# A graph network of four layers: two stages change the order of their work

## The chip, the cores and the metric

The kernel runs on one core of a Trainium2 chip. The core has five engines with a queue of instructions each: TensorE (PE; the loading of its weights is listed apart as PEld), VectorE (DVE), ScalarE (ACT), GpSimd (POOL) and SyncE (SP), which here only issues transfers. The engines work side by side and wait for one another by semaphores. The metric is the device time of one execution in microseconds (us); lower is better.

## The reference

There are 16 graphs of 1024 nodes with 256 features each, and a dense matrix `adj` of 1024 x 1024 weights per graph. Each of the four layers normalizes the features of a node (mean 0, variance 1), cuts them off below 0, computes something from the result `h` and `adj`, and adds that to `x`:

```python
# layer 0: attention whose weights are adj * exp(e_i + f_j + a_b), divided by their row sums
x = x + (u / u.sum(-1)) @ (h @ W_w.T + W_b)          # u = adj * exp(...)
# layer 1: graph convolution
d = (adj.sum(-1) + 1e-5) ** -0.5
x = x + (d[:, :, None] * adj * d[:, None, :]) @ (h @ weight) + bias
# layer 2: a gated recurrence over the 1024 nodes of a graph, one node after the other
# layer 3: neighbour sums, a wide inner layer with RMS norm and silu
agg = epsilon * h + adj @ h
t = agg @ W1 + b1                                     # inner width 1024
t = silu(t * rsqrt(mean(t * t) + 1e-6) * rms_weight)
x = x + t @ W2 + b2
```

All arithmetic is float32. A float32 product on TensorE is made of two instructions, so that counts of matmuls in the profile are twice those in the code.

## The kernel before

The program has three parts, one after the other: layers 0 and 1 together, layer 2, layer 3. Only the first and the last are changed; layer 2 takes the middle of the time and is the same in both versions. Between the parts, `x2_d`, `he_d`, `heT_d` and `hn_d` carry results through HBM. A graph is called a batch below. `NT` = 8 blocks of 128 nodes, `DC` = 2 halves of the features, `HC` = 8 blocks of the inner width.

**Layers 0 and 1.** `load` brings x (1 MB) and the transposed `adj` (`at`, 4 MB in four transfers) of a batch. `prepare` takes the statistics of x (`stats`, lines 128 to 136), forms the cut-off rows `q` (L176), the products `f` (L178), the exponentials `g` (L182) and scales q (L187). `layer_0` first multiplies `at` by g and by ones (`pd`, L196), which gives the row sums; then come the neighbour sums of q (`sums`, L152, 64 instructions with four results `pa`), the products with the weights (L214) and the addition to x (L215). `reshape` takes the statistics of the new x and forms the rows `h1` (L144). `layer_1` has the neighbour sums of h1, the products (L251), the addition (L252), the statistics of that and the rows `h2`, which leave for HBM. `turn` transposes h2 (L268). The loop interleaves these: in step i stand layer 0 of batch i, the transposes of batch i-2, and layer 1 of batch i-1, and in the pauses between the four neighbour sums of the latter the statistics of batch i (`reshape`) and the preparation of batch i+1.

**Layer 3.** For each batch: load x, hn and `at`; add epsilon to the diagonal of `at` (GpSimd, L683); x + hn (L684); normalize and cut off (L76 to L83); add b2 to x (GpSimd, L687); neighbour sums (L693), which come out with the features on partitions (`ag`). Then twice, for 512 nodes: the inner layer with the nodes on partitions (`ph`, L706), b1 added (L709), squares with their sum (L711), the root mean square (`rms`, L68), the scaling (L717), the transposes back (`pt`, L721) with silu (L722), and the products with W2 (L726) added to x (L727).

**What sets the order.** The kernel is written in a framework with a planner that orders the instructions before the program runs. By its own estimates of times it gives each engine the first instruction in program order whose inputs and buffers are there; so an instruction can overtake earlier ones of its engine that have to wait. In the chip's run that order is fixed, and each engine works through it strictly in order. Tiles are buffers with a name and a pool; a name has a fixed number (`bufs`) of them, which go round. `mv` has 2, `s6` 4 (L132), `pa` 2, `pmm` 2 in the first part.

Of the kernel before, what the change touches and what calls it, by code (L numbers as in the profile page):

```python
# [9 lines left out]
F32 = mybir.dt.float32  # L10
# [6 lines left out]
P = 128  # L17
# [21 lines left out]
def gnn_stack(ctx: ExitStack, tc: tile.TileContext, a: dict, out: bass.AP):  # L39
# [51 lines left out]


    def layers_0_1():
        with ExitStack() as st:
            wp = st.enter_context(tc.tile_pool(name="w01", bufs=1))
            big = st.enter_context(tc.tile_pool(name="big01", bufs=1))
# [41 lines left out]
            def normed(x, scale, mv, name, bufs):  # L138

                shift = small.tile([P, NT], F32, name="shift")  # L140
                nc.vector.scalar_tensor_tensor(shift, mv[:, :, 0], -1.0, scale, op0=ALU.mult, op1=ALU.mult)
                h = big.tile([P, NT, D], F32, name=name, bufs=bufs)
                for t in range(NT):
                    nc.scalar.activation(h[:, t], x[:, t], AF.Relu, bias=shift[:, t : t + 1], scale=scale[:, t : t + 1])  # L144
                return h

            def sums(at, h, ag):

                def part(n0, c):
                    pa = psum.tile([P, 512], F32, name="pa")  # L150
                    for mt in range(NT):
                        nc.tensor.matmul(pa, h[:, mt, c * P : (c + 1) * P], at[:, mt, n0 : n0 + 512],  # L152
                                         start=mt == 0, stop=mt == NT - 1)
                    if c == 0:
                        nc.scalar.copy(ag[:, c, n0 : n0 + 512], pa)
                    else:
                        nc.vector.tensor_copy(ag[:, c, n0 : n0 + 512], pa)  # L157
                return [lambda n0=n0, c=c: part(n0, c) for n0 in (0, 512) for c in range(DC)]

            at, x, q, g, h1, h2, dis = {}, {}, {}, {}, {}, {}, {}  # L160

            def load(b):
                x[b] = big.tile([P, NT, D], F32, name="x", bufs=4)
                nc.sync.dma_start(x[b], rows(a["x"][b]))
                at[b] = big.tile([P, NT, N], F32, name="at", bufs=3)
                for t in range(0, NT, 2):
                    nc.sync.dma_start(at[b][:, t : t + 2], rows(a["adjT"][b])[:, t : t + 2])

            def prepare(b):

                mv, rs = stats(x[b])
                yield
                q[b] = big.tile([P, NT, D], F32, name="q")
                f = small.tile([P, NT], F32, name="f")
                for t in range(NT):
                    nc.vector.tensor_scalar(q[b][:, t], x[b][:, t], mv[:, t, 0:1], 0.0, op0=ALU.subtract, op1=ALU.max)  # L176
                    junk = small.tile([P, D], F32, name="junk")
                    nc.vector.scalar_tensor_tensor(junk, q[b][:, t], rs[:, t : t + 1], v[:, :D],  # L178
                                                   op0=ALU.mult, op1=ALU.mult, accum_out=f[:, t : t + 1])
                    nc.gpsimd.tensor_tensor(x[b][:, t], x[b][:, t], vec["W_b"], ALU.add)  # L180
                g[b] = gs[b % 2]
                nc.scalar.activation(g[b][:, :, 0], f, AF.Exp, bias=v[:, D : D + 1])  # L182
                yield
                rg = small.tile([P, NT], F32, name="rg")
                nc.vector.tensor_mul(rg, rs, g[b][:, :, 0])
                for t in range(NT):
                    nc.scalar.activation(q[b][:, t], q[b][:, t], AF.Copy, scale=rg[:, t : t + 1])  # L187
                yield

            def layer_0(b, between):  # L190
                ds = big.tile([P, N], F32, name="ds")
                for n0 in (0, 512):
                    pd = psum.tile([P, 512], F32, name="pd")
                    for mt in range(NT):
                        k = mt % 4
                        nc.tensor.matmul(pd[32 * k : 32 * (k + 1)], g[b][:, mt], at[b][:, mt, n0 : n0 + 512],  # L196
                                         start=mt < 4, stop=mt >= 4)
                    nc.scalar.copy(ds[:, n0 : n0 + 512], pd)
                ag = big.tile([P, DC, N], F32, name="ag", bufs=2)
                for part in sums(at[b], q[b], ag):  # L200
                    part()
                    if between:
                        between.pop(0)()
# [6 lines left out]
                nc.vector.tensor_copy(deg, pn[:, :, 1])  # L210
                for nt in range(NT):
                    po = psum.tile([P, D], F32, name="pmm")
                    for c in range(DC):
                        nc.tensor.matmul(po, ag[:, c, nt * P : (nt + 1) * P], w0[:, c], start=c == 0, stop=c == DC - 1)  # L214
                    nc.vector.scalar_tensor_tensor(x[b][:, nt], po, rc[:, nt : nt + 1], x[b][:, nt],  # L215
                                                   op0=ALU.mult, op1=ALU.add)

                dis[b] = inv_sqrt(small, deg, DEG_EPS, [P, NT], "dis")
# [7 lines left out]
                return safe  # L226

            def reshape(b, safe):

# [5 lines left out]
                mv, rs = stats(x[b])  # L235
                rd = small.tile([P, NT], F32, name="rd")
                nc.vector.tensor_mul(rd, rs, dis[b])
                h1[b] = normed(x[b], rd, mv, "h1", 2)
                for t in range(NT):
                    nc.gpsimd.tensor_tensor(x[b][:, t], x[b][:, t], vec["bias"], ALU.add)  # L240

            def layer_1(b, between):
                ag = big.tile([P, DC, N], F32, name="ag", bufs=2)
                for part in sums(at[b], h1[b], ag):
                    part()
                    if between:
                        between.pop(0)()
                for nt in range(NT):
# [3 lines left out]
                    nc.vector.scalar_tensor_tensor(x[b][:, nt], po, dis[b][:, nt : nt + 1], x[b][:, nt],  # L252
                                                   op0=ALU.mult, op1=ALU.add)
                nc.gpsimd.dma_start(rows(x2_d[b]), x[b])

                mv, rs = stats(x[b])
                h2[b] = normed(x[b], rs, mv, "h2", 1)
                nc.gpsimd.dma_start(rows(he_d[b]), h2[b])

            def turn(b):  # L260

                hT = big.tile([P, DC, N], F32, name="hT")

                def part(c):
                    for t0 in range(0, NT, 4):
                        pt = psum.tile([P, 512], F32, name="pt")
                        for t in range(4):
                            nc.tensor.transpose(pt[:, t * P : (t + 1) * P], h2[b][:, t0 + t, c * P : (c + 1) * P], ident)  # L268
# [4 lines left out]
                    if c == DC - 1:  # L273
                        nc.gpsimd.dma_start(heT_d[b], hT)
                return [lambda: part(0), lambda: part(1)]

            nothing = lambda: None
            load(0)
            for _ in prepare(0):
                pass  # L280
            for i in range(B + 2):
                if i + 1 < B:
                    load(i + 1)
                turns = [nothing] + turn(i - 2) if i >= 2 else []
                if i < B:
                    safe = layer_0(i, turns)
                for part in turns:
                    part()
                between = []
                if i < B:  # L290
                    between.append(lambda: reshape(i, safe))
                if i + 1 < B:
                    rows_of = prepare(i + 1)
                    between += [lambda: next(rows_of)] * 3
                if 1 <= i <= B:
                    layer_1(i - 1, between)
                for part in between:
                    part()
# [350 lines left out]

    def layer_3():  # L650
        with ExitStack() as st:
# [8 lines left out]
            nc.sync.dma_start(w2, a["W2"].rearrange("(c p) e -> p c e", p=P))  # L660
            rw = wp.tile([P, HC], F32, name="rw")
            with nc.allow_non_contiguous_dma(reason="weights, once"):
                nc.sync.dma_start(rw, a["rms_weight"].rearrange("(c p) -> p c", p=P))
            b1 = wp.tile([P, H], F32, name="b1")
            nc.sync.dma_start(b1, bcast_row(a["b1"], H))  # L665
# [7 lines left out]
            NH = 512  # L673
            for b in range(B):
                at = big.tile([P, NT, N], F32, name="at")
                x = big.tile([P, NT, D], F32, name="x")
                hn = big.tile([P, NT, D], F32, name="hn", bufs=1)
                nc.sync.dma_start(x, rows(x2_d[b]))
                nc.sync.dma_start(hn, rows(hn_d[b]))  # L679
                for t in range(0, NT, 2):  # L680
                    nc.sync.dma_start(at[:, t : t + 2], rows(a["adjT"][b])[:, t : t + 2])  # L681
                for t in range(NT):
                    nc.gpsimd.tensor_tensor(at[:, t, t * P : (t + 1) * P], at[:, t, t * P : (t + 1) * P], eye, ALU.add)  # L683
                nc.vector.tensor_add(x, x, hn)  # L684
                h = ln_relu(small, big, x)
                for t in range(NT):
                    nc.gpsimd.tensor_tensor(x[:, t], x[:, t], b2, ALU.add)  # L687
                ag = big.tile([P, DC, N], F32, name="ag", bufs=1)
                for n0 in range(0, N, NH):
                    for c in range(DC):  # L690
                        pa = psum.tile([P, NH], F32, name="pa")
                        for mt in range(NT):
# [89 lines left out]
```

## Time and profile before

| | |
|---|---|
| median of 3 runs | 6928.25 us (6926.89 to 6928.35) |
| profiled execution, its own time | 6928.25 us |
| its span in the profile | 6926.5 us |
| TensorE busy, instructions | 6482.0 us (94%), 28325 |
| layers 0 and 1, first `pd` to last transpose | 27.57 to 1327.6 us |
| layer 3, first neighbour sum to the end | 5332.75 to 6926.5 us |
| mean granted TensorE clock | 0.968 |

The profile is that of one execution. Times in its views count from the start of the span. A group line has the line of the code and the engine, the operation, the tiles written and read, shapes and count; then busy time, the mean of one in ns, and the idle time of the engine before it with what ended it. A line in order of time begins with start and duration in us. The duration of one matmul overlaps with the next one, so the rate of a row of them is read from the starts. A line of windows gives, for each stretch, the busy time of the engines, the clock that TensorE was granted as a fraction of the full one, the busy share of the 16 DMA engines and GB/s.

### The profile page before, as it was taken

To read this page: it belongs to the slowest core of one execution; us is meant where nothing else is said; L and a number is where in the kernel's file an instruction comes from. 1 tells how busy PE (TensorE), PEld (TensorE's weight loads), DVE (VectorE), ACT (ScalarE), POOL (GpSimd) and SP (SyncE) were. 2 spreads that over 40 slices of the span, in tenths; PEclk is the share of its full clock that TensorE was granted. 3 is DMA by queue.
4 is the path that set the end of the run, shared out by engine and by line. 5 is a ranking of instruction groups with operands and counts; after the bars stand their busy time and mean duration, and the time that the engine had idled before them with its cause. 6 is when DMAs were issued, how large, how long until landed. Compare 5 with 4: busy or idle time off the path is not lost. (4 is left out here: it accounts for less than half of the span.)

```text
span 6926.5 us, 72473 instructions
## 1 busy us (share of the span) xinstructions
PE 6482.0 (94%) x28325; PEld 4703.9 (68%) x28325; DVE 2475.9 (36%) x5926; ACT 1447.6 (21%) x3211; POOL 894.6 (13%) x1299
## 2 busy tenths in 40 slices
PE   7999999679999999999999999999998999999998
PEld 3455545378878878788788788788785555555555
DVE  4444444213333333333333333333333233323332
ACT  1211222102212212112112122122122222222222
POOL 2222322110000000100100100000001111111110
PEclk9999999899999999999999999999999999999999
DMA  3322222371131132221221222211003122212210
GB/s 120 121 105 99 98 97 98 95 210 56 62 87 49 60 88 63 65 72 52 63 74 61 73 65 62 82 49 49 22 6 109 65 79 85 69 66 78 85 55 13
DMA packets 477363, 520.77 MB, mean 75 GB/s; under 512 B 30208, under 2 KB 428800, under 8 KB 474752
## 3 DMA queue, kind: packets, MB, share of 16 engines
q1 hardware_dynamic: 461056, 447.93, 20.2%
q0 software_dynamic: 15872, 67.18, 2.6%
q8 instruction: 256, 4.19, 0.3%
q14 instruction: 179, 1.47, 0.1%
HBM read 431.10 MB, written 83.95 MB: 74 GB/s over the span
## 5 line engine op out<-in xcount | busy, mean ns | idle before, releaser
L401 PEld LDWEIGHTS pb<-ab,hb 128*128 128x128 f32 x3648 | 522.8, 195 | 89.1 <-issue 34.3
L401 PE MATMUL pb<-ab,hb 128*128 128x128 f32 x3648 | 533.8, 280 | 50.2 <-DMA hb<-he_d 30.5
L551 PE MATMUL pa<-wh,r 128*128 128x256 f32 x2080 | 494.2, 380 | 0.0
L152 PE MATMUL pa<-at,h 128*128 128x512 f32 x1024 | 459.1, 603 | 34.9 <-DVE ag L157 34.9
L693 PE MATMUL pa<-at,h 128*128 128x512 f32 x1024 | 444.3, 595 | 31.5 <-ACT h L83 31.5
L726 PE MATMUL pa<-w,hT 128*128 128x256 f32 x2048 | 468.1, 384 | 0.0
L539 ACT ACTIVATE r<-pr 128x256 f32<-128x256 f32 x520 | 199.2, 383 | 1230.1 <-PE pr L536 1217.5
L706 PE MATMUL ph<-w,ag 128*128 128x512 f32 x1024 | 452.7, 593 | 0.0
L152 PE MATMUL pa<-at,q 128*128 128x512 f32 x1024 | 448.4, 594 | 0.0
L551 PEld LDWEIGHTS pa<-wh,r 128*128 128x128 f32 x2080 | 387.2, 191 | 74.7 <-issue 22.9
L726 PEld LDWEIGHTS pa<-w,hT 128*128 128x128 f32 x2048 | 385.3, 193 | 46.5
L152 PEld LDWEIGHTS pa<-at,h 128*128 128x128 f32 x1024 | 195.2, 193 | 272.0 <-issue 223.9
L693 PEld LDWEIGHTS pa<-at,h 128*128 128x128 f32 x1024 | 195.6, 191 | 270.9 <-issue 267.4
L536 PE MATMUL pr<-x,wh 128*128 128x256 f32 x1568 | 372.7, 380 | 0.0
L543 PE MATMUL pz<-wh,x 128*128 128x256 f32 x1568 | 370.5, 379 | 0.0
L562 DVE TENSOR_TENSOR w<-w,hc 128x256 f32<-128x256 f32 x520 | 236.2, 454 | 370.8 <-ACT hc L561 370.8
L540 DVE TENSOR_TENSOR r<-r,x 128x256 f32<-128x256 f32 x392 | 167.0, 426 | 542.8 <-ACT r L539 541.7
L152 PEld LDWEIGHTS pa<-at,q 128*128 128x128 f32 x1024 | 191.5, 190 | 236.9 <-issue 236.9
L706 PEld LDWEIGHTS ph<-w,ag 128*128 128x128 f32 x1024 | 191.2, 190 | 214.8 <-issue 214.0
L543 PEld LDWEIGHTS pz<-wh,x 128*128 128x128 f32 x1568 | 298.4, 190 | 40.0
L536 PEld LDWEIGHTS pr<-x,wh 128*128 128x128 f32 x1568 | 292.3, 191 | 43.5 <-issue 3.3
L561 ACT ACTIVATE hc<-pa 128x256 f32<-128x256 f32 x520 | 196.2, 383 | 538.4 <-PE pa L551 538.3
(154 smaller groups left out, 9573.8 us busy)
## 6 DMA issues: line engine op xcount, KB each, us to landing
at<-in_adjT SPq DMA_DIRECT2D x128, 1024.0 KB
ab<-in_adj SPq DMA_DIRECT2D x128, 512.0 KB
x<-in_x SPq DMA_DIRECT2D x16, 1024.0 KB
x_d<-x POOLq DMA_DIRECT2D x16, 1024.0 KB, 7.7
he_d<-h POOLq DMA_DIRECT2D x16, 1024.0 KB, 8.6
heT_d<-hT POOLq DMA_DIRECT2D x16, 1024.0 KB, 4.2
he<-heT_d SPq DMA_DIRECT2D x16, 1024.0 KB
hb<-he_d SPq DMA_DIRECT2D x16, 1024.0 KB
```

The lines of the kernel that those rows point to most:

```text
L152: nc.tensor.matmul(pa, h[:, mt, c * P : (c + 1) * P], at[:, mt, n0 : n0 + 512], start=mt == 0, stop=mt == NT - 1)
L401: nc.tensor.matmul(pb[:, c], hb[:, j, c * P : (c + 1) * P], ab[:, j], start=j == jts[0], stop=j == jts[-1])
L536: nc.tensor.matmul(prs[e], wh[:, c, e * P : (e + 1) * P], x[:, c], start=False, stop=c == DC - 1)
L539: nc.scalar.activation(r[:, e], prs[e], AF.Sigmoid)
L540: nc.vector.tensor_mul(r[:, e], r[:, e], x[:, e])
L543: nc.tensor.matmul(pz[:, g], x[:, c, g * GR : (g + 1) * GR], wh[:, c, D : 2 * D], start=False, stop=g == G2 - 1 and c == DC - 1)
L551: nc.tensor.matmul(pcs[g], r[:, c, g * GR : (g + 1) * GR], wh[:, c, 2 * D :], start=False, stop=c == DC - 1)
L561: nc.scalar.activation(hc[:, g], pcs[g], AF.Tanh)
L562: nc.vector.tensor_mul(w[:, g], w[:, g], hc[:, g])
L693: nc.tensor.matmul(pa, h[:, mt, c * P : (c + 1) * P], at[:, mt, n0 : n0 + NH], start=mt == 0, stop=mt == NT - 1)
L706: nc.tensor.matmul(ph, ag[:, c, (t0 + t) * P : (t0 + t + 1) * P], w1[:, c, e * 512 : (e + 1) * 512], start=c == 0, stop=c == DC - 1)
L726: nc.tensor.matmul(po, hT[:, k, t * P : (t + 1) * P], w2[:, k], start=k == 0, stop=k == HC - 1)
```

## The change

Two parts are changed. In layers 0 and 1 the interleaving is taken out: one loop over the batches does everything for a batch in order. `x`, `at`, `q`, `ag` and the rest have two buffers each, and x1 and x2 are tiles of their own. The operations and their shapes stay the same.

In layer 3, `inner` computes the inner layer with its features on partitions, so that nothing has to be transposed; b1 and the RMS weight become a column per block. The mean over the inner width is then one over partitions and blocks: ScalarE squares each block, GpSimd adds the eight blocks up (`ss`), TensorE sums that over the partitions by a product with a column of ones (`mean`), and spreads the reciprocal root over the partitions by transposes of a broadcast column (`spread`). VectorE multiplies, ScalarE applies silu (`apply`). The neighbour sums of the next batch stand in four pieces between these, and loads and preparation run two batches ahead.

```diff
@@ layers_0_1 @@
-            big = st.enter_context(tc.tile_pool(name="big01", bufs=1))
+            big = st.enter_context(tc.tile_pool(name="big01", bufs=2))
...
+            for b in range(B):
+                at = big.tile([P, NT, N], F32, name="at")
+                x = big.tile([P, NT, D], F32, name="x")
+                nc.sync.dma_start(x, rows(a["x"][b]))
                 for t in range(0, NT, 2):
+                    nc.sync.dma_start(at[:, t : t + 2], rows(a["adjT"][b])[:, t : t + 2])
...
+                mv, rs = stats(x)
+                q = big.tile([P, NT, D], F32, name="q")
...
+                ag = summed(at, q)
...
+                x1 = big.tile([P, NT, D], F32, name="x1")
...
+                mv, rs = stats(x1)
                 rd = small.tile([P, NT], F32, name="rd")
+                nc.vector.tensor_mul(rd, rs, dis)
+                h = normed(x1, rd, mv, "h")
...
+                ag = summed(at, h)
+                x2 = big.tile([P, NT, D], F32, name="x2")
...
+                nc.gpsimd.dma_start(rows(x2_d[b]), x2)
...
+                mv, rs = stats(x2)
+                h = normed(x2, rs, mv, "h")
+                nc.gpsimd.dma_start(rows(he_d[b]), h)
                 hT = big.tile([P, DC, N], F32, name="hT")
...
-            for i in range(B + 2):
-                if i + 1 < B:
-                    load(i + 1)
-                turns = [nothing] + turn(i - 2) if i >= 2 else []
-                if i < B:
-                    safe = layer_0(i, turns)
...
-                if 1 <= i <= B:
-                    layer_1(i - 1, between)
...
@@ layer_3 @@
-            b1 = wp.tile([P, H], F32, name="b1")
-            nc.sync.dma_start(b1, bcast_row(a["b1"], H))
+            b1 = wp.tile([P, HC], F32, name="b1")
...
+            def load(b):
+                x[b] = big.tile([P, NT, D], F32, name="x", bufs=3)
+                hn[b] = big.tile([P, NT, D], F32, name="hn", bufs=1)
...
+            def prepare(b):
+                for t in range(NT):
+                    nc.gpsimd.tensor_tensor(at[b][:, t, t * P : (t + 1) * P], at[b][:, t, t * P : (t + 1) * P], eye, ALU.add)
+                nc.vector.tensor_add(x[b], x[b], hn[b])
+                h[b] = ln_relu(small, big, x[b])
+                for t in range(NT):
+                    nc.gpsimd.tensor_tensor(x[b][:, t], x[b][:, t], b2, ALU.add)
...
+            def inner(ag, n0, between):
+
+                hh = big.tile([P, HC, NH], F32, name="hh")
+                ss = small.tile([P, NH], F32, name="ss")
+                for k in range(HC):
+                    ph = psum.tile([P, NH], F32, name="ph")
+                    for c in range(DC):
+                        nc.tensor.matmul(ph, w1[:, c, k * P : (k + 1) * P], ag[:, c, n0 : n0 + NH],
+                                         start=c == 0, stop=c == DC - 1)
+                    sq = ss if k == 0 else small.tile([P, NH], F32, name="sq")
+                    nc.scalar.activation(sq, ph, AF.Square, bias=b1[:, k : k + 1])
+                    nc.vector.tensor_scalar(hh[:, k], ph, b1[:, k : k + 1], None, op0=ALU.add)
+                    if k:
+                        nc.gpsimd.tensor_tensor(ss, ss, sq, ALU.add)
+                    if k in between:
+                        between[k]()
+                return hh, ss
+
+            def norm(hh, ss):
+
+                got = {}
+
+                def mean():
+                    pq = psum.tile([P, NH // P], F32, name="pq", bufs=1)
+                    for n in range(NH // P):
+                        nc.tensor.matmul(pq[:, n : n + 1], ss[:, n * P : (n + 1) * P], ones[:, 0:1], start=True, stop=True)
+                    got["rms"] = inv_sqrt(small, pq, RMS_EPS, [P, NH // P], "rms", mul=1.0 / H)
+
+                def spread():
+                    pr = psum.tile([P, NH], F32, name="pr", bufs=1)
+                    for n in range(NH // P):
+                        nc.tensor.transpose(pr[:, n * P : (n + 1) * P], got["rms"][:, n : n + 1].to_broadcast([P, P]), ident)
+                    got["pr"] = pr
+
+                def apply(quarter):
+                    for k in (2 * quarter, 2 * quarter + 1):
+                        nc.vector.tensor_mul(hh[:, k], hh[:, k], got["pr"])
+                        nc.scalar.activation(hh[:, k], hh[:, k], AF.Silu, scale=rw[:, k : k + 1])
+                return mean, spread, apply
...
+                hh0, ss0 = inner(ag, 0, {})
+                mean0, spread0, apply0 = norm(hh0, ss0)
+                hh1, ss1 = inner(ag, NH, {1: mean0, 4: spread0})
+                mean1, spread1, apply1 = norm(hh1, ss1)
+                parts = [lambda: None] * 4
+                if b + 1 < B:
+                    ag, parts = sums(b + 1)
+                for k in range(4):
+                    apply0(k)
+                parts[0]()
+                mean1()
+                parts[1]()
+                spread1()
+                outer(b, hh0, 0, apply1)
+                parts[2]()
+                if b + 2 < B:
+                    prepare(b + 2)
+                parts[3]()
+                outer(b, hh1, NH)
+                nc.gpsimd.dma_start(rows(out[b]), x[b])
```

## The prediction

> **What bounds the kernel now.** I read the page's busy shares first, then the windows of one steady batch in layers 0/1 and one in layer 3, then the order in time on TensorE, then the groups.
>
> ```profile
> PE 6482.0 (94%) x28325; PEld 4703.9 (68%) x28325; DVE 2475.9 (36%) x5926; ACT 1447.6 (21%) x3211; POOL 894.6 (13%) x1299
> 602.41:681.35 78.94, 76.48 (x259) 40.09 (x258) 37.00 (x110) 15.95 (x33) 21.64 (x24) 1.00 0.28 107
> 5532.94:5631.92 98.98, 93.78 (x322) 56.51 (x321) 32.60 (x64) 25.74 (x58) 13.99 (x20) 0.97 0.22 75
> ```
>
> TensorE sets the time. In the windows the columns are stretch, length, busy time of PE, PEld, DVE, ACT, POOL, then clock and DMA. A batch takes 78.94 us in layers 0/1, with TensorE 97% busy at clock 1.00, and 98.98 us in layer 3 at 0.97. So layers 0/1 have almost nothing to win and much to lose; layer 3 has its transposes and gaps to win. TensorE in time order shows what an uninterleaved batch costs. The kernel's own first batch is one:
>
> ```profile
> 62.93 7.45 PE L214 MATMUL pmm<-w,ag 128*128 128x256 f32 x32
> 70.21 0.27 PE L231 MATMUL pt<-ident,safe 128*8 128x128 f32 x1
> 90.97 5.18 PE L196 MATMUL pd<-at,gs 128*32 128x512 f32 x32 [20.48 <-ACT gs L182]
> 96.08 27.73 PE L152 MATMUL pa<-at,q 128*128 128x512 f32 x64
> ...
> 641.41 7.11 PE L251 MATMUL pmm<-w,ag 128*128 128x256 f32 x32
> 648.45 3.64 PE L196 MATMUL pd<-at,gs 128*32 128x512 f32 x32
> ```
>
> After batch 0's layer 0, TensorE idles 20.48 us until batch 1's exp (gs) is done. In the steady state the same `pd` follows the last product with no gap. Why did nothing run ahead? VectorE:
>
> ```profile
> 47.69 0.69 DVE L157 COPY ag<-pa 128x512 f32<-128x512 f32 x1 [19.97 <-PE pa L152]
> 61.42 0.69 DVE L157 COPY ag<-pa 128x512 f32<-128x512 f32 x1 [13.04 <-PE pa L152]
> 72.42 0.38 DVE L133 BATCH_NORM_STATS2 s<-x 128x6 f32<-128x256 f32 x1
> ```
>
> The transfers of x[1] had ended by about 52 us (the DMA strip is at 0 from there), VectorE idled, yet batch 1's statistics start only behind batch 0's second ones at 71 us. The planner does fill gaps out of program order elsewhere, so this is a buffer: `s6` (4 buffers) and `mv` go round in program order, and later statistics queue behind earlier ones.
>
> **What the skill says.** "SBUF — State Buffer", Who interferes with whom: VectorE collides with GpSimd only with two SBUF inputs or in a 2-port mode. The trace agrees: L709 (one PSUM input) takes 689 ns under GpSimd work, 691 without; L178 (two SBUF inputs) 1237 against 474. "TensorE: Matmul & The Clock Gate", Part 1: an idle window of about 3.4 us halves the clock until about 3.4 us of work have passed. The windows agree: 0.50 from 73.6 to 91.0 us, 0.54 from 91.0 to 94.4, then 1.00; `pd` then takes 5.11 us to its successor instead of 3.57, so a long stall costs 1.5 us more. "Perfetto Trace Analysis", Optimization Strategy: consistent bubbles can mean no buffer for the next tile; that is my reading of 71 us.
>
> **Part 1, layers 0/1 go back to one batch after the other.** Statistics are now, in program order, x, x1, x2 of batch b, then x of b+1, all through the 4 buffers of `s6`. So x of b+1 can't be prepared before x2 of b has its statistics, after b's last product. Two stalls appear per batch.
>
> Stall A, layer 0 to layer 1: last L215, statistics, power on GpSimd (1.66), shift, first ACT row. Batch 0 shows it: L214 ends 70.4, the rows start at 74.73 and the first takes 0.5: 4.8 us, plus 1.5 of clock = 6.3. The first matmuls of b+1 can't fill it: they need the exp that comes later.
>
> Stall B, layer 1 to the next batch: 1.3 us until x2's statistics are done; then what the start of the kernel shows undisturbed, from first statistics (12.89) to `pd` (27.57), 14.7; added 0.6 for x2's power input and shift on VectorE, 1.3 for two 0.69 us hT copies, about 1.1 for a DMA issue on GpSimd (0.94) that holds VectorE up: 19.0. From above, the 20.48 just shown contains a heavier GpSimd load (8 bias adds). I keep 16.5 to 21.5. The 16 transposes of h lie inside B.
>
> Period: pd 5.1 + sums 27.55 + pn 1.70 + products 7.44 + A 6.3 + sums 27.47 + products 7.0 + B 19.0 = 101.6 us. The first batch starts at 27.57 as now; its last product ends 27.57 + 83.6 + 15 x 101.6 = 1635.2, against 1317.2 now: **+318 us**, 80% between 275 and 355. Loads stay hidden: `at` goes from 3 buffers to 2, but its buffer frees at the end of the sums of b-1, some 90 us before use, and 4 MB land in 11 us (the `eye` adds follow its quarters every 2.5). Layer 2's first loads wait for the last heT_d in both; what follows is unmoved, apart from the order layer 3's few weights come in (512 KB of b1 less, under 3 us).
>
> **Part 2, layer 3.** Durations on TensorE per batch now: sums 27.47, ph 2 x 13.75, products 128 x 0.2159 = 27.63; 64 transposes x 0.109 = 7.0; the rest to 98.98, 9.4, is waits and half clock. Removed: the transposes, both waits for `rms` (work of the next batch stands there), ACT's accumulator reads. Added on TensorE: 8 one-column products of 2 instructions at 0.106 (rate of L206) 1.7, and 8 transposes 0.9. Floor: 27.47 + 27.5 + 27.63 + 2.6 = 85.2.
>
> Other engines per k of `inner` (1.72 us of TensorE): ACT Square 0.6, VectorE bias 0.69, GpSimd one 128x512 add.
>
> ```profile
> L423 POOL TENSOR_TENSOR ao<-ao,dv 128x512 f32<-128x512 f32 x28 | 35.6, 1270 | 182.0 <-DMA ao<-in_adj 176.2 <-PE pb L427 5.8
> L687 POOL TENSOR_TENSOR x<-x,b 128x256 f32<-128x256 f32 x128 | 94.5, 771 | 8.5 <-DVE h L81 8.5
> L684 DVE TENSOR_TENSOR x<-x,hn 128x2048 f32<-128x2048 f32 x16 | 36.8, 2303 | 164.7 <-DMA x<-x_d 154.4 <-DMA hn<-hn_d 10.3
> ```
>
> An add of 512 costs 1.27 (L423) to 1.40 (line through 0.455 for 128 and 0.771 for 256); I take 1.35. ("GPSIMD Engine Reference", 3.1, gives 2.6 cycles per element, an estimate of 1.27 with its dispatch.) That is under 1.72, so GpSimd keeps up, but its slack of 0.37 is thin: the 8 `eye` adds (0.455), 8 b2 adds (0.77) and powers of a later batch want the same engine, and an `eye` add whose `at` lands late holds the sums queued behind it; then `sq` (2) and `ph` (2) fill and TensorE waits. The x+hn add (2.3 us, two SBUF inputs, longer beside GpSimd) can hold VectorE's bias adds likewise, over the 1.72 that two `ph` cover. The output's DMA issue on GpSimd (0.93) waits for the batch's last product; behind it stands the next batch's first add, which is due 3.5 us later: hidden. On SP, x of b+2 waits for the output of b-1 to leave its buffer, `at` behind it: about 22 us into a batch, 40 before use. The silu and multiplications of the second half lie under 13.8 us of products; if `rms` were late, TensorE would still have a part of 6.87 us. I charge 3 us a batch, between 0 (all fits) and 8 (GpSimd queue in the wrong order). Period 88.2.
>
> Layer 3 now: 5332.75 to 6919.0 = 1586.3. After: first sums 29.7, 15 x 88.2, last batch, which has no sums to cover its waits, 57.7 + 5.5: 1415.9. **-170 us**, at the floor -217.
>
> **Sum.** On the profiled execution, span 6926.5: + 318 - 170 = 7074.5. Its own time is 6928.25, 1.75 above the span and equal to the median of the runs: 7076. I put 7075.
>
> **Rivals.**
> 1. Layer 3 at its floor: 6926.5 + 318 - 217 + 1.75 = 7029. For it: DVE and ACT are a third busy. Against: the planner hoists the next batch's preparation into the inner loops, as it did at 5742 us.
> 2. Layer 3 gains nothing, GpSimd is the bound: a batch at 98 us has 12.8 us over the floor, so the inner loops take 40 us instead of 27.5; 14 adds, with 16 `eye` and b2 adds (9.8 us) among them, fill that at 2.2 us an add. Then layer 3 takes about 1581, in all about 7240. Against: L423's 1.27.
> 3. The other side: the planner prepares b+1 early after all, since every tile has two buffers now. Then B vanishes and A is partly filled by `pd`; the period is about 81, layers 0/1 end 9 us later, and the time is 6926.5 + 9 - 170 + 2 = 6768. It turns at a B of 9 us: (318 - 170)/15 = 9.9 less than my 19. Against it: the 71 us reading, in a stretch with the same 4 `s6` buffers.
> The change may also not interleave as written, if the planner moves the neighbour sums; that ends between rivals 1 and 2.
>
> **How the numbers follow.** Main case 0.62 (own range 7025 to 7130), rival 1 0.22, rival 2 0.08, rival 3 0.08. The range 7005 to 7145 holds the main case but for its tails and rival 1. Within 0.2% is 14 us, about what a measurement here can tell. Faster 0.07 (rival 3), same 0.03 (B and layer 3 both at their good ends), slower 0.90.
>
> **What would show it.** Right: in layers 0/1 `pd` waits 15 to 20 us for the exp once per batch and the h sums 4 to 5 us for ACT; PEclk falls below 0.95 there; 16 periods of 100 us. In layer 3 no L721 transposes, PE above 96%, period 85 to 91. Wrong: statistics of the next x before x2's, no wait before `pd`; or GpSimd busy without gaps in `inner` and `ph` waiting on it.

## The result

The changed kernel takes 7038.23 us (median of 4 runs, 7033.98 to 7045.41), the kernel before beside it 6927.57 us (6922.5 to 6928.35): a ratio of 1.0162, interval 1.0145 to 1.018. It is slower by 110.7 us. The prediction said 7075 with a range of 7005 to 7145.

The profiled execution has a span of 7032.3 us against 6926.5, 105.8 more. By stages, read from the matmuls of each stage on TensorE (us; the periods are means without the first batch):

| | before | after | after - before | predicted |
|---|---|---|---|---|
| layers 0/1, start to last transpose | 1327.5 | 1606.7 | +279.2 | +318 |
| period of a batch there | 79.6 | 98.99 | +19.4 | 101.6 |
| layer 2 (code unchanged) | 3973.3 | 3954.8 | -18.5 | 0 |
| layer 3, first neighbour sum to last product | 1586.2 | 1431.7 | -154.5 | -170 |
| period of a batch there | 98.98 | 89.4 | -9.6 | 88.2 |

The rest, -0.4, lies in the gap ahead of layer 3, behind the last product and in rounding. Layer 2 executes the same code, with its instructions in the same order on TensorE, VectorE, ScalarE and GpSimd. In the thirteen kernels profiled beside the one before it took between 3954.8 and 3969.0 us, each time less than the 3973.3 of the kernel before. By the medians too about 14 us lie outside the two changed stages (279.2 - 154.5 is 124.7, measured are 110.7). Why layer 2 is shorter stays open; that the change has no part in it isn't shown.

The page of the changed kernel, busy times and then the granted clock in 40 slices:

```profile
PE 6479.6 (92%) x27685; PEld 4632.5 (66%) x27685; DVE 2461.0 (35%) x6022; ACT 1438.9 (20%) x2955; POOL 1196.2 (17%) x1523
PEclk9889898987999999999999999999999999999999
```

TensorE is busy for as long as before, although it has 640 instructions fewer. The clock row fits that: in the first nine slices, which are layers 0/1, it falls to 8 again and again. The windows of one steady batch, first in layers 0/1, then in layer 3 (length, busy PE, PEld, DVE, ACT, POOL, clock, DMA):

```profile
523.00:622.00 99.00, 84.66 (x261) 42.33 (x265) 32.26 (x111) 16.13 (x33) 21.56 (x24) 0.90 0.23 85
6211.00:6300.40 89.40, 86.92 (x278) 50.01 (x278) 35.52 (x71) 24.96 (x42) 33.42 (x34) 1.00 0.22 83
```

In layers 0/1 TensorE now stands for 14.3 us of a batch and runs at 0.90 (76.48 busy of 78.94 at 1.00 before). In layer 3 it is 97% busy at full clock (95% at 0.97 before). Where it stands in layers 0/1, TensorE in order of time:

```profile
599.05 7.27 PE L233 MATMUL pmm<-w,ag 128*128 128x256 f32 x32
611.32 5.88 PE L247 MATMUL pt<-ident,h 128*128 128x128 f32 x16 [5.00 <-ACT h L142]
621.93 5.09 PE L188 MATMUL pd<-at,gs 128*32 128x512 f32 x32 [4.74 <-ACT gs L178]
626.95 27.73 PE L152 MATMUL pa<-at,q 128*128 128x512 f32 x64
654.52 1.84 PE L194 MATMUL pmm<-sel,ds 128*128 128x2 f32 x16
656.22 7.46 PE L203 MATMUL pmm<-w,ag 128*128 128x256 f32 x32
663.52 0.27 PE L216 MATMUL pt<-ident,safe 128*8 128x128 f32 x1
668.29 29.90 PE L152 MATMUL pa<-at,h 128*128 128x512 f32 x64 [4.50 <-ACT h L142]
```

Stall B goes from the end of the products of layer 1 (606.32) to `pd` (621.93): 15.6 us, of which 5.9 are the transposes. Stall A is 4.50 us of idling ahead of the sums of h, and the sums that follow take 29.7 instead of 27.5 us. VectorE at the start of B:

```profile
606.43 0.48 DVE L234 SCALAR_TENSOR_TENSOR x<-pmm,dis,x 128x256 f32<-128x256 f32 x1
606.83 0.17 DVE L132 BATCH_NORM_AGGREGATE mv<-s 128x2 f32<-128x6 f32 x1
606.95 0.75 DVE L131 BATCH_NORM_STATS2 s<-x 128x6 f32<-128x256 f32 x2
...
613.58 0.94 DVE L174 SCALAR_TENSOR_TENSOR junk<-q,rs,v 128x256 f32<-128x256 f32 x1 [1.53 <-POOL rs L68]
```

Of the two statistics at 606.95 the first is the last one of x2, since it needs the addition before it; the second, at 607.29, is the first one of the next batch. The input of that batch has long been there, yet its statistics begin directly behind the last ones of x2. This is what the prediction said of the order; whether its cause, the buffers, is right, the line can't say.

In layer 3 the transposes (L721 of the code before) are gone, and the groups of the inner loop read:

```profile
L671 PE MATMUL ph<-ag,w 128*128 128x512 f32 x1024 | 481.1, 613 | 34.1 <-DVE hh L675 33.9
L677 POOL TENSOR_TENSOR ss<-ss,sq 128x512 f32<-128x512 f32 x224 | 304.7, 1360 | 117.6 <-ACT sq L674 113.2
```

TensorE waits 33.9 us, 2.1 a batch, for VectorE's bias addition. GpSimd's addition of squares takes 1360 ns on average, and GpSimd is the one that waits there (113.2 us, for ScalarE; the other way round, ScalarE waits 44.6 us for GpSimd).

### The profile page after: what moved, and what is told of

The parts are those of the page before. It is cut to its first block, busy times and chain, and to the rows that moved or that the text cites. A ratio compares the mean times of both kernels' runs of the same rounds, so it can differ in the third digit from the quotient of the medians.

```text
span 7032.3 us, 71626 instructions
## 1 busy us (share of the span) xinstructions
PE 6479.6 (92%) x27685; PEld 4632.5 (66%) x27685; DVE 2461.0 (35%) x6022; ACT 1438.9 (20%) x2955; POOL 1196.2 (17%) x1523
## 5 line engine op out<-in xcount | busy, mean ns | idle before, releaser
L355 PEld LDWEIGHTS pb<-ab,hb 128*128 128x128 f32 x3648 | 525.1, 196 | 89.4 <-issue 37.6
L152 PE MATMUL pa<-at,h 128*128 128x512 f32 x1024 | 478.3, 631 | 72.0 <-ACT h L142 72.0
L671 PE MATMUL ph<-ag,w 128*128 128x512 f32 x1024 | 481.1, 613 | 34.1 <-DVE hh L675 33.9
L656 PE MATMUL pa<-at,h 128*128 128x512 f32 x1024 | 455.8, 596 | 31.3 <-DMA at<-in_adjT 31.3
L709 PE MATMUL po<-w,hh 128*128 128x256 f32 x2048 | 447.7, 379 | 0.0
L709 PEld LDWEIGHTS po<-w,hh 128*128 128x128 f32 x2048 | 388.4, 190 | 58.7 <-issue 7.9
L157 DVE COPY ag<-pa 128x512 f32<-128x512 f32 x64 | 44.3, 692 | 980.4 <-PE pa L152 980.4
L671 PEld LDWEIGHTS ph<-ag,w 128*128 128x128 f32 x1024 | 179.7, 191 | 295.6 <-DVE hh L675 151.3
L677 POOL TENSOR_TENSOR ss<-ss,sq 128x512 f32<-128x512 f32 x224 | 304.7, 1360 | 117.6 <-ACT sq L674 113.2
```

What stands on the lines that cost most here:

```text
L355: nc.tensor.matmul(pb[:, c], hb[:, j, c * P : (c + 1) * P], ab[:, j], start=j == jts[0], stop=j == jts[-1])
L656: nc.tensor.matmul(pa, h[b][:, mt, c * P : (c + 1) * P], at[b][:, mt, n0 : n0 + NH], start=mt == 0, stop=mt == NT - 1)
L671: nc.tensor.matmul(ph, w1[:, c, k * P : (k + 1) * P], ag[:, c, n0 : n0 + NH], start=c == 0, stop=c == DC - 1)
L677: nc.gpsimd.tensor_tensor(ss, ss, sq, ALU.add)
L709: nc.tensor.matmul(po, hh[:, c, k * P : (k + 1) * P], w2[:, c], start=c == 0, stop=c == HC - 1)
```

## The experiments

### One part at a time

Theory: the two parts are independent, and their sum is the result. Rival: one part helps or harms the other, through the loads or through layer 2.

`l01_only` has the new layers 0/1 and the old layer 3.

> Layers 0 and 1 of the changed kernel with layer 3 of the kernel before. Theory (the two parts add up): layers 0 and 1 with a period of 99.0 us as in the changed kernel, layer 3 with one of 98.98: +279 us on the kernel before, less whatever made layer 2 18 us shorter in the changed kernel's profile: 7190 to 7207 us. Rival (the parts act on each other, for example through transfers or placement of buffers): outside 7180 to 7215.

Measured: 7205.56 us, ratio 1.0401 (1.0384 to 1.0419). Period 98.99, layers 0/1 end at 1607.6, layer 3 takes 1586.4.

`l3_only` has the old layers 0/1 and the new layer 3.

> Layer 3 of the changed kernel with layers 0 and 1 of the kernel before. Theory: the interleaved first stage keeps its 78.9 us a batch, layer 3 has 89.4: 155 us less than before, 6755 to 6773 us, with the lower end if layer 2's 18 us come from layer 3's side of the program and the upper if they come from the first stage or from the run. Rival: outside 6745 to 6783.

Measured: 6762.97 us, ratio 0.9763 (0.9747 to 0.978). Layers 0/1 end at 1327.4, layer 3 takes 1429.3.

Against the kernel before in the same session (6928.77) that is +276.8 and -165.8, together +111.0; both at once gave +110.7. The parts add up, and each stage takes the same in either company. So layer 3's new form is a gain of 2.4% that the first part more than takes back. Which part of that form brings how much (the transposes that are gone, the work of the next batch in the gaps) wasn't tried apart. In the windows, a batch of layer 3 has 6.9 us less of busy TensorE (93.78 to 86.92) and 2.7 us less of idling (5.20 to 2.48).

### What holds the next batch's statistics back

The prediction's cause was the number of buffers: four of `s6`, two of `mv`. First the number of `s6` alone:

```diff
-                    s6 = small.tile([P, 6], F32, name="s6", bufs=4)
+                    s6 = small.tile([P, 6], F32, name="s6", bufs=16)
```

> The changed kernel with 16 buffers of s6 instead of 4, nothing else. Theory (stall B exists because the small statistics tile goes round in program order): the next batch's statistics and exp run during the neighbour sums, pd follows the last product without a wait, and also fills most of stall A: a period of 78 to 82 us instead of 99.0, so 6730 to 6790 us. Rival 1 (buffers are given out strictly in program order, so mv and rs hold it back as well): no change, 7038 us. Rival 2 (no buffer at all, the planner doesn't look that far ahead): no change, and none with names of their own either.

Measured: 7035.79 us (1.0155, 1.0138 to 1.0172), period 98.99. Nothing moved. Then `after_many`: 16 of `s6`, and 8 each of `mv`, `rs` and `rs_v`, still one name each for the statistics of x, x1 and x2.

> The changed kernel with 16 buffers of s6 and 8 of mv, rs and rs_v (4, 2, 2, 2 before), names shared as in the changed kernel. If what holds the next batch's statistics is the number of buffers, the wait before pd goes and the time is 6730 to 6790 us, as with names of their own. If buffers of one name are given out strictly in program order, so that a later tile waits for an earlier one to get its buffer however many are free, nothing changes: period 99.0 us, 7025 to 7050 us.

Measured: 7037.8 us in one run, period 98.99. With four times the buffers the next batch still waits. Then `after_names`: the numbers as in the changed kernel, but names of their own for the tiles of x's statistics.

```diff
-            def stats(x):
+            def stats(x, own=""):
...
-                mv = small.tile([P, NT, 2], F32, name="mv")
+                mv = small.tile([P, NT, 2], F32, name="mv" + own)
...
-                    s6 = small.tile([P, 6], F32, name="s6", bufs=4)
+                    s6 = small.tile([P, 6], F32, name="s6" + own, bufs=4)
...
-                rs = inv_sqrt(small, mv[:, :, 1], LN_EPS, [P, NT], "rs")
+                rs = inv_sqrt(small, mv[:, :, 1], LN_EPS, [P, NT], "rs" + own)
...
-                mv, rs = stats(x)
+                mv, rs = stats(x, "0")
```

> The changed kernel with names of their own (mv0, s60, rs0) for the statistics of a batch's first x, so that they share no buffers with those of x1 and x2. Theory and rival 1 of the run with 16 buffers: the wait before pd goes, period 78 to 82 us, 6730 to 6790 us. Rival 2 (no buffer): 7038 us. If this run is fast and the other isn't, mv or rs is what holds; if both are, s6 alone is.

Measured: 6748.36 us (0.974, 0.9724 to 0.9756). The period is 79.53, about that of the kernel before (79.6) with its interleaving written by hand. TensorE, with the 27685 instructions of the changed kernel, is busy for 6384.2 us instead of 6479.6. In order of time:

```profile
579.03 7.12 PE L233 MATMUL pmm<-w,ag 128*128 128x256 f32 x32
586.07 1.06 PE L188 MATMUL pd<-at,gs 128*32 128x512 f32 x6
587.06 5.42 PE L152 MATMUL pa<-at,q 128*128 128x512 f32 x12
...
626.50 2.78 PE L188 MATMUL pd<-at,gs 128*32 128x512 f32 x24
630.98 27.73 PE L152 MATMUL pa<-at,h 128*128 128x512 f32 x64 [1.70 <-ACT h L142]
```

The first `pd` stands directly behind the products (stall B is gone), the rest of the next batch's `pd` fills A (626.50) but for 1.70 us, and the sums of h run at full clock. This is the picture of the prediction's rival 3, at the price of four names (`rs0` brings `rs0_v` with it).

Which name counts? `s60_only` gives only `s6` a second one:

> As the changed kernel, but only the statistics tile s6 of x has a name of its own (s60); mv, rs and rs_v still share theirs. If every shared name holds the statistics of the next x back by itself: period 98.99 in layers 0/1, time as the changed kernel's, 7033 to 7045. If s6 alone was what held (the prediction's first suspect): period 79.5 and 6745 to 6752, as with all names apart. If mv is asked for at the start of the statistics and s6 is not what counts, the same 98.99.

Measured: 7035.32 us in one run, period 98.99. `names_rs_shared` gives `s6` and `mv` a second one, and leaves `rs` and `rs_v` shared:

> As the changed kernel, with names of their own for x's s6 and mv, while rs and rs_v stay shared by the three statistics. If each name holds back only the step that asks for it: x of the next batch gets its statistics and q early, its rs only behind x2's; then the f chain starts about 2.9 us earlier than at 613.58 and the period falls to 95 to 97, time 6985 to 7010. If any shared name holds the whole: 98.99 and 7033 to 7045. If rs doesn't matter: 79.5 and 6745 to 6752.

Measured: 6938.97 us in one run, period 92.3 (median). The statistics run early, as expected, and `rs` only behind x2's; but the gain on the changed kernel is 99 us where 28 to 53 were expected, so the size was missed. TensorE, then VectorE, in order of time:

```profile
567.14 7.27 PE L233 MATMUL pmm<-w,ag 128*128 128x256 f32 x32
579.01 5.88 PE L247 MATMUL pt<-ident,h 128*128 128x128 f32 x16 [4.59 <-ACT h L142]
584.81 4.11 PE L188 MATMUL pd<-at,gs 128*32 128x512 f32 x32
```

```profile
575.72 0.55 DVE L64 TENSOR_SCALAR rs_v<-mv 128x8 f32<-128x8 f32 x2
578.10 0.17 DVE L139 SCALAR_TENSOR_TENSOR shift<-mv,rs 128x8 f32<-128x8 f32 x1 [1.84 <-POOL rs L68]
579.70 0.48 DVE L174 SCALAR_TENSOR_TENSOR junk<-q,rs,v 128x256 f32<-128x256 f32 x1 [1.44 <-POOL rs L68]
```

The statistics and q of the next batch now run early, and the two `rs_v` (575.72, x2) wait for x2's statistics together. From the end of the products to the first L174 it is 5.3 us (574.41 to 579.70), 7.3 in the changed kernel (606.32 to 613.58). Beyond what was expected, an L174 takes 0.48 us instead of 0.94 (GpSimd's additions of `W_b` no longer run beside it), and q lies outside the chain too. And `pd`, now directly behind the transposes, takes 4.05 us to its successor instead of 5.02.

So sharing `rs` and `rs_v` holds back the power and what needs it, and sharing `mv` as well holds back the statistics. The order in which they run is the order of the code, and more buffers don't loosen it. That the planner hands out the buffers of one name strictly in program order fits all the periods (99.0 in each kernel that shares the names or parts only `s6`, 92.3, 79.53). It remains an inference from these runs: the planner's code wasn't read, and a name of its own for `mv` alone wasn't tried, so whether `s6` needs one isn't known.

### What is left in layer 3

The charge for stalls was 3 us above a floor of 85.2; the period is 89.4. In the last batch but one, where nothing is loaded or prepared for a later batch, it is 86.1, and no wait of TensorE is listed in it: loads and preparation cost 3.3 of the 4.2. TensorE in a batch with a preparation, the waits alone:

```profile
6275.28 1.99 PE L671 MATMUL ph<-ag,w 128*128 128x512 f32 x4 [0.38 <-DVE hh L675]
...
6278.23 1.98 PE L671 MATMUL ph<-ag,w 128*128 128x512 f32 x4 [0.86 <-DVE hh L675]
...
6283.04 1.99 PE L671 MATMUL ph<-ag,w 128*128 128x512 f32 x4 [0.67 <-DVE hh L675]
...
6286.32 1.98 PE L671 MATMUL ph<-ag,w 128*128 128x512 f32 x4 [0.43 <-DVE hh L675]
```

That is 2.3 us, all for the bias addition. Three suspects were tried on `after_names`, whose layer 3 takes 1430.9 us. The chain of work that ended last, in the changed kernel (start, duration, instruction), names the first, GpSimd's additions of b2:

```profile
6366.71 2.40 POOL x L647 x4
6369.11 0.48 issue
6369.60 1.27 POOL ss L677
...
6374.90 0.76 DVE hh L675
6375.66 0.04 issue
6375.70 1.98 PE ph L671 x4
```

`names_no_b2` leaves the addition of b2 out:

> The kernel with statistics under names of their own (6748 us), without layer 3's 8 additions of b2 a batch on GpSimd: part of the computation is left out. Theory (the preparation's adds on GpSimd hold up the sums of squares, which hold Square, which holds ph): most of the 3.3 us that a batch with a preparation takes beyond one without (89.4 against 86.1) goes, period 86.5 to 88, layer 3 in all 20 to 45 us less than 1431. Rival (VectorE is what holds ph): under 10 us less.

Measured: 6735.86 us (0.9725, 0.9708 to 0.9741); layer 3 takes 1417.7, 13.2 less, with a period of 88.6. That lies between the 20 to 45 of the theory and the under 10 of the rival: the suspect is real, but its share of the 4.2 is 0.8, and most of the 3.3 is something else. The second suspect is the x + hn addition, which holds VectorE for 2.3 us:

```diff
-                nc.vector.tensor_add(x[b], x[b], hn[b])
+                for t in range(NT):
+                    nc.vector.tensor_add(x[b][:, t], x[b][:, t], hn[b][:, t])
```

> The kernel with statistics under names of their own (6748 us), with layer 3's x+hn as 8 adds of 256 columns in place of one of 2048. Theory (GpSimd is what holds): the 2.3 us block on VectorE is gone but was mostly covered, 0 to 10 us less in layer 3. Rival (VectorE's long instruction holds the bias adds and ph): 20 to 40 us less. Eight instructions cost about 1 us more of VectorE a batch.

Measured: 6779.74 us (0.9785, 0.9769 to 0.9801), layer 3 takes 1464.4, 33.5 **more**, period 91.8. A miss in sign. The groups of the step behind that addition, the rows of h, in `names_xhn8` and in `after_names` (durations in ns: least, median, most):

```profile
L81 DVE TENSOR_SCALAR h<-x,mv,rs x88: 400/814/1378, 5638.1 to 6575.8; 128x256 f32<-128x256 f32 x88
```

```profile
L81 DVE TENSOR_SCALAR h<-x,mv,rs x88: 402/411/1415, 5631.7 to 6531.6; 128x256 f32<-128x256 f32 x88
```

In pieces the addition and the statistics end later (`rs_v` 22.4 us after the batch's first `ph`, 19.2 in `after_names`), and the order changes: more of the h rows run beside a GpSimd addition and take over 0.5 us (85 of 128, against 56). The eight rows of a batch take 6.3 us in sum, 5.2 in `after_names`. VectorE there, in order of time, with TensorE's wait behind it:

```profile
5822.45 1.67 DVE L81 TENSOR_SCALAR h<-x,mv,rs 128x256 f32<-128x256 f32 x2 [1.76 <-POOL rs L68]
5824.04 0.74 DVE L676 TENSOR_SCALAR hh<-ph,b 128x512 f32<-128x512 f32 x1
```

```profile
5824.84 3.66 PE L672 MATMUL ph<-ag,w 128*128 128x512 f32 x4 [2.54 <-DVE hh L676]
```

VectorE waits for GpSimd's power with a bias addition queued behind it; TensorE waits 2.54 us, and the next `ph` takes 3.66 instead of 1.98. These two come to 4.2 us in this batch, where all the waits shown above were 2.3; the period grew by 2.4. The wait for the power alone is no longer than in `after_names` (28.2 and 28.3 us over layer 3), so it is the place of the rows that differs.

The third suspect is that the bias addition waits for ScalarE's Square of the same `ph` (114.2 us of waiting in the changed kernel from 5600 us on). "PSUM — Partial Sum Buffer", PSUM bank collisions raise a hardware error, in the Trainium skill says that ScalarE and VectorE must not read one bank of the same partitions at once, and that the compiler adds a dependency. The trace agrees: none of the 256 bias additions starts earlier than 0.03 us after the end of its Square. `names_sq_hh` lets Square read the result of the bias addition instead:

```diff
-                    nc.scalar.activation(sq, ph, AF.Square, bias=b1[:, k : k + 1])
                     nc.vector.tensor_scalar(hh[:, k], ph, b1[:, k : k + 1], None, op0=ALU.add)
+                    nc.scalar.activation(sq, hh[:, k], AF.Square)
```

> The kernel with statistics under names of their own (6748 us); ScalarE squares hh, which VectorE has written to SBUF, in place of ph plus bias. In the changed kernel VectorE's bias add waits for ScalarE's Square of the same ph (114 us of waits), so a ph is held for both, one after the other, about 1.7 us; here only for the bias add, about 1 us. Theory (ph is held too long): TensorE's waits for ph, 2.3 us a batch, go, 20 to 35 us less in layer 3. Rival (GpSimd holds sq, and Square waits all the same, but no longer with ph): a similar gain, and GpSimd's lag then shows at the mean, where pq waits for ss. If neither: no change.

Measured: 6743.15 us (0.9733, 0.9717 to 0.9749), layer 3 1425.8, 5.1 less; most of the expected gain isn't there. The bias addition no longer waits for Square. But here too the median L81 is 811 ns, VectorE waits 36.8 us for `rs` between 5300 and 6700 us instead of 28.3, and TensorE still waits 2.8 us a batch for the bias addition: the row got another hold-up in place of the old one.

### A version that is faster than both

GpSimd's b2 additions can be done by VectorE in the pauses between the products with W2, where it idles 3.03 us each time:

```diff
-                for t in range(NT):
-                    nc.gpsimd.tensor_tensor(x[b][:, t], x[b][:, t], b2, ALU.add)
...
+                    nc.vector.tensor_add(x[b][:, t], x[b][:, t], b2)
                     nc.vector.tensor_add(x[b][:, t], x[b][:, t], po)
```

> All names apart, and layer 3's b2 added by VectorE ahead of the addition of po, not by GpSimd in the preparation; everything is computed. VectorE is idle 3.03 us between po additions, an add of 128x256 with two SBUF inputs takes about 0.4: hidden, also from the last batch's end but for 0.4. If GpSimd's b2 adds cost what their removal showed: layer 3 as without them, 1417 to 1420, time 6733 to 6741. If VectorE's adds get into the bias adds: period 89 or more, 6745 to 6755.

Measured: 6731.07 us (6728.1 to 6739.69), 0.9723 of before (0.9707 to 0.9739), and by the medians 0.956 of the changed kernel. Layer 3 takes 1417.8, the same as without b2: hidden entirely. What remains is again VectorE. Of the four h rows at 5886.36 the two in the middle take 1.36 and 1.42 us, beside GpSimd's additions of squares, the others 0.40:

```profile
5886.36 3.35 DVE L81 TENSOR_SCALAR h<-x,mv,rs 128x256 f32<-128x256 f32 x4
5889.62 0.74 DVE L673 TENSOR_SCALAR hh<-ph,b 128x512 f32<-128x512 f32 x1
```

```profile
5886.61 2.62 POOL L675 TENSOR_TENSOR ss<-ss,sq 128x512 f32<-128x512 f32 x2
```

```profile
5890.42 1.98 PE L669 MATMUL ph<-ag,w 128*128 128x512 f32 x4 [1.83 <-DVE hh L673]
```

`names_b2v_sq` adds the third suspect's edit:

> As before, and Square reads hh in SBUF. If the two gains (13.2 and 5.1 us of layer 3) add up: layer 3 1412 to 1415, time 6728 to 6736. If both shorten the same wait for the bias add: layer 3 1415 to 1422, time 6733 to 6742.

Measured: 6737.29 us (0.9728, 0.9712 to 0.9744), layer 3 1423.0. The gains don't add up. The time lies in the range expected if both shorten the same wait, but layer 3 lies 1.0 above its range and is 5.2 longer than with b2 moved alone. The steady period is 88.75 instead of 88.61, and the first batch (91.5 instead of 90.3) and one later batch (90.5) are longer too; why isn't explained.

## Why the prediction was right, and where it was not

**Direction and place.** Right: each part acted in the direction that was said, and independently of the other. The forecast of 7075 was 37 too high. By the traces: layers 0/1 39 too high, the time of layer 3 15 too low, and layer 2 18.5 shorter in the profiled execution, which no step of the prediction dealt with. That the errors of the two parts have opposite signs, and that the total came as near as it did, is luck. As the medians have it, +276.8 and -165.8 where +318 and -170 were said; these differences hold whatever shortens layer 2.

**Part 1, the period.** The terms, predicted and measured: `pd` 5.1 and 5.02; sums 27.55 and 27.57; pn 1.70 and 1.70; products 7.44 + 7.0 and 7.30 + 7.27; A's idling 4.8 and 4.77 (663.52 to 668.29); sums of h 27.47, with 1.5 of clock, and 29.74; B 19.0 and 15.6. The sum is 98.99 where 101.6 was said, and 15 times the 2.6 between them is the 39 us. (Two sums of the prediction don't come out of their own terms: the first batch is 82.6, not 83.6, where 83.7 was measured, and the floor of layer 3 gives -215, not -217. Neither moves the forecast by more than 2 us.)

The term mis-sized is **stall B**. Its 1.3 + 14.7 + 0.6 + 1.3 + 1.1 added up parts that overlap. The 1.3 ahead of the next batch's statistics is 1.0 (606.32 to 607.29). From the first of these to `pd` it takes 14.6 us, which is the undisturbed 14.7, without the 3.0 that were added to it: x2's power runs on GpSimd while VectorE already has x's statistics, the hT copies come behind the f chain (after 621 us), and on GpSimd the DMA issues of the batch (607.21 and 619.98 in its row) end when x2's power is due, at 608.2, or come after the power of x. Work that ran at the same time was priced as if it stood in one row. The clock term of A was too small the other way, 2.3 for 1.5: the 1.5 was taken from a `pd` row, and the sums of h lose more behind a stall that is shorter (their window, at a clock of 0.93):

```profile
668.29:698.00 29.71, 29.71 (x64) 13.08 (x65) 0.69 (x1) 4.56 (x9) 5.50 (x8) 0.93 0.02 8
```

**The cause of B.** The step that named "`s6` (4 buffers) and `mv`" going "round in program order" was half right. Program order by name fits every run; more buffers change nothing (4 or 16 of `s6`, 2 or 8 of `mv`, `rs` and `rs_v` gave the same period). The reading at 71 us showed a wait that followed program order; that it was for want of buffers was an inference, and it carried the argument against rival 3. The stalls came as forecast because the three statistics share their names, not because their buffers are few; so the step was right in the order and wrong in its reason. It was rival 3 that described what happens once the names are apart, and it came at 79.53 where about 81 was said.

**Part 2.** The floor of 85.2 was reached: in `names_sq_hh` the one batch without preparation took 85.2, in the changed kernel 86.1. The charge of 3 was 4.2. 1.27 us for an undisturbed addition of squares (the median is 1267 ns) was right, 1.35 for the mean too (1360). Rival 2, GpSimd as the bound, falls: it waits for ScalarE in the inner loop, and layer 3 gained. Of what the charge named as threats, the b2 additions cost 0.8 a batch (shown by taking them out). The share of the x + hn addition no run shows; beside it one addition of squares took 3.17 us, the longest of all 224 (6263.94, two in 4.51):

```profile
6263.69 2.29 DVE L644 TENSOR_TENSOR x<-x,hn 128x2048 f32<-128x2048 f32 x1 [0.89 <-DMA x<-x_d]
```

```profile
6263.94 4.51 POOL L677 TENSOR_TENSOR ss<-ss,sq 128x512 f32<-128x512 f32 x2 [0.51 <-ACT sq L674]
```

Not foreseen was the row in which Square, bias addition and the next batch's h rows stand, with a wait for GpSimd's power in the middle. In every variant TensorE's waits in the inner loops of a steady batch are for the bias addition in this row (between 2.2 and about 4.4 us a batch), but for one of 0.22 us for GpSimd in `names_xhn8`. That this is why the gains don't add up, and that the row is the whole of the remaining 3.4 us, is argued from the waits and not shown by a run without it.

## What to carry to other kernels

When work of a later stage could run early and doesn't, look at which tile names the two share before counting their buffers: here names of their own for four small tiles were worth 290 us of 7038, and 16 buffers of one of them instead of 4 nothing. A stall that is made of work on several engines need not be the sum of that work; here the undisturbed run of the same chain was the better estimate, and the extras belonged in the upper end of the range. And on an engine that others wait for, cutting up a long instruction can cost more than it frees, since it moves what stands behind it.

## What the runs showed of the hardware

- A VectorE instruction that collides with a GpSimd addition takes about as long as that addition, however short it is alone. L174 takes 0.48 us alone and 0.94 beside an addition of `W_b` (256 columns, 0.8 us). L81 takes 0.41 alone, 0.81 beside an addition of b2 (256 columns, about 0.8) and 1.36 to 1.42 beside one of squares (512 columns, 1.27). Beside GpSimd's power `rms` (6275.11 to 6276.23 in the changed kernel) L81 stays at 0.41. "SBUF — State Buffer", Who interferes with whom, in the Trainium skill gives the ports that the two engines share, held by one of them at a time, as the reason. The durations agree with such a lock. The other side pays as well: GpSimd's 1.27 us addition took 3.17 beside the x + hn addition of 2.29.
- Behind a pause of 4.5 us on TensorE the 27.5 us of sums took 2.3 us more, at a granted clock of 0.93; behind one of 1.70 us, in `after_names`, they took 27.6. In layers 0/1, where three such pauses come to a batch (5.00, 4.74 and 4.50 us above), the clock was granted at 0.90 over the batch, and at 1.00 over a batch of the same stage in `after_names`, where the 1.70 us are the only pause.
- Cutting a VectorE addition of 2048 columns into eight of 256, with no other edit, made the kernel 31 us slower (`names_xhn8` against `after_names`); more of the rows behind it then ran beside GpSimd's additions.
